# Later stages of a group woven into the absolute differences of the next

## The chip, the cores and the metric

The kernel runs on one core of a Trainium2 chip. The metric is the device time of one execution in microseconds, the median over runs; the profile is one execution of its own.

## The reference

The input is 16 images of 32 channels of 128 x 128 float32. Four layers follow one another, each of the form x = x + f(norm(x)), where norm is a group norm over pairs of channels of one image:

```python
x = x + _L0(_gn(x))   # diagonal LSTM: 128 steps along the width, state shifted by a row at each
x = x + _L1(_gn(x))   # 3x3 "adder" convolution: -sum over (c, kh, kw) of |q(patch) - q(w)|, 32 outputs
x = x + _L2(_gn(x))   # Hartley transform, 32 x 32 modes mixed over channels, inverse transform
x = x + _L3(_gn(x))   # five edge operators, each normalised over its image; conv1, pool, conv2, pool,
                      # conv3, pool, conv4, deconv, conv5, deconv, conv6, deconv, conv7; x * that
```

In L1 x and w are quantised to whole numbers from -127 to 127. In L3 `orig * y` is returned, with `orig` the normalised input.

## The kernel before

The kernel works in stages, one after another, over the whole batch; the images go through HBM between them (x1, x2, x3).

`stage0` runs the recurrence, with the batch on partitions in four groups (`NG = 4`) of four images.

`stage1` computes the absolute differences. An image is first normalised and quantised (`quantise`) to 16-bit floats in HBM (`q_d`), and loaded half by half (`loaded`, 64 rows), four copies over the partitions, so that partition = (one of 4 outputs, channel). For each half there are 72 steps `i` = (one of 8 blocks of outputs, one of 9 taps). A step makes max(q - w, 0) as a tile of 128 x 8192, on ScalarE where `i % 4 == 3` (line 365, tile `d_act`, 2 buffers), else on VectorE (line 367, `d_dve`, 4 buffers). Then 16 matmuls (line 372) with a selection matrix sum it over channels into four PSUM banks `acc`. A linear term of 9 x 16 matmuls (line 347) opens the sum of a half, since |a| = 2 max(a, 0) - a. `finish` (lines 324 and 326) adds the residual from the four banks, takes statistics and stores x2; it is called at `i == 3` of the next half. There are 4 such banks, so the linear term of a half waits for `finish` of the half before.

`stage2` is the transform: for 16 images two matmul rounds (lines 426 and 432), the modes through HBM, the mixing (line 467), through HBM again, and for each group two inverse rounds (lines 506 and 526) with the residual added in a ring of 4 tiles `xr2`.

`encoder_decoder` works by groups. `frames.chunk` loads 20 rows of x3 into a ring of 4 tiles `xp` and normalises them (line 664). `edge_statistics` forms Gram products over 128 rows (line 693) for the mean and deviation of the five operators; `fold_operators` folds the operators into conv1's weights. The function `prepared(g + 1)` stands ahead of conv1 of group g. conv1 runs 25 taps for each of 8 chunks (line 952), with pooling (line 853) and the bias into y1 (lines 862 and 864, alternately on VectorE and ScalarE); then conv2 to conv6 (lines 840 and 612), the last two composed with the deconvolutions (`Composed`). `last_layer` does the third deconvolution with conv7 (line 612 again), the scaling (lines 1032, 1041, 1044) and the output.

All instructions are emitted in the order of the program text; a scheduler then orders them per engine and places the waits. Loads go mostly through SP's queue, some stores and weights through ScalarE's.

Of the kernel before, what the change touches and what calls it, by code (L numbers as in the profile page):

```python
# [209 lines left out]
def jc_stats(nc, pool, ps, cst, v, name):  # L210

    rhs = pool.tile([128, NG, 4], F32, name=f"{name}_r")
    nc.vector.tensor_tensor(rhs, bcast(v[:, :], 2, 4), bcast(cst["m4_bc"], 1, NG), ALU.mult)
    p = ps.tile([128, 512], F32, name="acc")
    nc.tensor.matmul(p[:, :16], cst["sel_c"], rhs.rearrange("p g b -> p (g b)"), start=True, stop=True)
    out = pool.tile([128, 16], F32, name=name)
    nc.vector.tensor_copy(out, p[:, :16])
    return out


def jc_rows(t, b, half, n=16 * W):

    return bass.AP(t.tensor, t.offset + b * CHW + half * 64 * W, [[16 * W, 4], [HW, C], [1, n]])


def stage1(nc, tc, keep, cst, sel16, m1, r1, x1, w, q_d, x2):
# [8 lines left out]
    with ExitStack() as ctx:  # L235
        sm = ctx.enter_context(tc.tile_pool(name="s1_sm", bufs=1))
        with tc.tile_pool(name="s1_ps0", bufs=2, space=PSUM) as ps:
            r128 = jc_stats(nc, sm, ps, cst, r1, "r128")
            shift = jc_stats(nc, sm, ps, cst, m1, "shift")
            nc.vector.tensor_scalar(r128, r128, 128.0, None, ALU.mult)  # L240
            nc.vector.scalar_tensor_tensor(shift, shift, -1.0, r128, ALU.mult, ALU.mult)


            qw = sm.tile([128, 72], F32, name="qw")
            nc.sync.dma_start(qw, w)
            top = sm.tile([128, 1], F32, name="top")
            nc.vector.tensor_reduce(top, qw, AX.X, ALU.max, apply_absolute_value=True)
            alltop = sm.tile([128, 1], F32, name="alltop")
            nc.gpsimd.partition_all_reduce(alltop, top, 128, bass_isa.ReduceOp.max)
            scale = sm.tile([128, 1], F32, name="scale")  # L250
            nc.vector.tensor_scalar(scale, alltop, 1.0 / 127.0, 1e-8, ALU.mult, ALU.max)
            nc.vector.tensor_scalar(scale, scale, 2.0**0.5, None, ALU.mult)
            nc.vector.tensor_scalar(scale.bitcast(I32), scale.bitcast(I32), 0x7F800000, None, ALU.bitwise_and)
            nc.vector.reciprocal(scale, scale)
            nc.vector.tensor_scalar(qw, qw, scale, -127.0, ALU.mult, ALU.max)
            nc.vector.tensor_scalar(qw, qw, 127.0, RND, ALU.min, ALU.add)
            nc.vector.tensor_scalar(qw, qw, RND, None, ALU.subtract)
            neg = sm.tile([128, 72], F32, name="neg")
            nc.vector.tensor_scalar(neg, qw, -1.0, None, ALU.mult)


            taps = sm.tile([128, 8], F32, name="taps")
            nc.vector.tensor_reduce(taps, qw.rearrange("p (f t) -> p f t", t=9), AX.X, ALU.add)
            tapb = sm.tile([128, 8, 4], F32, name="tapb")
            nc.vector.tensor_tensor(tapb, bcast(taps[:, :], 2, 4), bcast(cst["m4_bc"], 1, 8), ALU.mult)
            sumw = sm.tile([128, 1], F32, name="sumw")
            p = ps.tile([128, 512], F32, name="acc")
            for j in range(4):
                nc.tensor.matmul(
                    p[32 * j : 32 * j + 32, :1],  # L270
                    tapb.rearrange("p f b -> p (f b)"),
                    cst["ones"][:, :1],
                    start=True,
                    stop=True,
                )
            nc.vector.tensor_scalar(sumw, p[:, :1], 2.0**-7, None, ALU.mult)

        stat = sm.tile([128, B, 8, 6], F32, name="stat2")
        ring = [sm.tile([128, 16, P], F16, name=f"qt{i}") for i in range(2)]
        for t in ring:  # L280
            nc.gpsimd.memset(t, 0.0)
        for row in (0, H + 1):
            nc.sync.dma_start(
                bass.AP(q_d.tensor, q_d.offset + row * P, [[4 * (H + 2) * P, 128], [(H + 2) * P, 4], [1, P]]),
                ring[0].rearrange("p r w -> p (r w)")[:, : 4 * P].rearrange("p (a w) -> p a w", w=P),
            )
        xp = ctx.enter_context(tc.tile_pool(name="s1_x", bufs=2))
        rp = ctx.enter_context(tc.tile_pool(name="s1_r", bufs=2))
        qp = ctx.enter_context(tc.tile_pool(name="s1_q", bufs=2))
        dp = ctx.enter_context(tc.tile_pool(name="s1_d", bufs=2))  # L290
        ps = ctx.enter_context(tc.tile_pool(name="s1_ps", bufs=4, space=PSUM))

        def unquantised(b, half):
            t = xp.tile([128, 16 * W], F32, name="xq")
            nc.sync.dma_start(t, jc_rows(x1, b, half))
            return t

        def quantise(b, half, t):
            nc.scalar.activation(
                t, t, AF.Identity, bias=shift[:, b : b + 1], scale=r128[:, b : b + 1]  # L300
            )
            qt = ring[half]
            nc.vector.tensor_scalar(
                qt[:, :, 1 : W + 1], t.rearrange("p (r w) -> p r w", w=W), RND, RND, ALU.add, ALU.subtract
            )
            flat = qt.rearrange("p r w -> p (r w)")
            nc.vector.tensor_scalar(flat, flat, -127.0, 127.0, ALU.max, ALU.min)
            first = q_d.offset + (b * C * (H + 2) + 64 * half + 1) * P
            nc.sync.dma_start(
                bass.AP(q_d.tensor, first, [[16 * P, 4], [(H + 2) * P, C], [1, 16 * P]]), flat  # L310
            )

        def loaded(b, half):
            q = qp.tile([128, R + 2, P], F16, name="q")
            first = q_d.offset + (b * C * (H + 2) + R * half) * P
            nc.sync.dma_start(q, bass.AP(q_d.tensor, first, [[0, 4], [(H + 2) * P, C], [1, (R + 2) * P]]))
            xr = rp.tile([128, 16 * W], F32, name="xr1")
            nc.sync.dma_start(xr, jc_rows(x1, b, half))
            return q, xr

        def finish(b, half, acc, xr):
            v = [xr[:, 512 * k : 512 * k + 512] for k in range(4)]
            for k in range(4):
                nc.vector.scalar_tensor_tensor(v[k], acc[k], sumw, v[k], ALU.subtract, ALU.add)  # L324
            for k in range(4):
                nc.vector.bn_stats(stat[:, b, 4 * half + k, :], v[k])
            nc.sync.dma_start(jc_rows(x2, b, half), xr)

        for half in range(2):
            quantise(0, half, unquantised(0, half))  # L330
        before = None
        following = loaded(0, 0)
        for b in range(B):
            for half in range(2):
                q, xr = following
                if (b, half) != (B - 1, 1):
                    following = loaded(b + half, 1 - half)
                if half == 0 and b + 1 < B:
                    xq = [unquantised(b + 1, i) for i in range(2)]
                acc = [ps.tile([128, 512], F32, name="acc") for _ in range(4)]  # L340
                for tap in range(9):
                    kh, kw = tap // 3, tap % 3
                    for j in range(4):
                        for k in range(4):
                            rows = slice(32 * k, 32 * k + 32)
                            row = 16 * j + 4 * k + kh
                            nc.tensor.matmul(  # L347
                                acc[k][32 * j : 32 * j + 32, :],
                                sel16[rows, 8, :],
                                q[rows, row : row + 4, kw : kw + W],  # L350
                                start=tap == 0,
                                stop=False,
                            )
                for i in range(72):
                    f8, tap = i // 9, i % 9
                    kh, kw = tap // 3, tap % 3
                    act = i % 4 == 3
                    if i == 3 and before:
                        finish(*before)
                    d = dp.tile([128, R, P], F16, name="d_act" if act else "d_dve", bufs=2 if act else 4)  # L360

                    src = q[:, kh : kh + R, :] if kw == 1 else q[:, kh : kh + R, kw : kw + W]
                    dst = d if kw == 1 else d[:, :, :W]
# [179 lines left out]
def replicated(nc, pool, src, n, name):  # L543
# [3 lines left out]
    return wr  # L547


class Composed:  # L550

# [44 lines left out]
    def round(self, src, n, acc, pick):  # L602
# [3 lines left out]
        for tap in range(4):  # L606
# [13 lines left out]
            if tap != 2:  # L620
                continue
# [577 lines left out]
```

## Time and profile before

| what | us |
|---|---|
| runs | 8965.4, 8966.56, 8978.64; median 8966.56 |
| profiled execution, its own time | 8964.56 |
| its span, first to last instruction | 8962.7 |
| stage0 and first quantisation, to the first difference | 0 to 1510 |
| absolute differences | 1510 to 5697 |
| transform | to 6450 |
| encoder and decoder | to 8558 |
| last layer | to 8962.7 |
| busy PE, DVE, ACT, POOL | 6114.4, 5850.7, 5003.2, 268.8 |

PE is TensorE, PEld its weight loads, DVE is VectorE, ACT ScalarE, POOL GpSimd, SP the engine that issues most DMAs. A group of the profile names the line, the engine, the operation, output and input tiles, the count, the busy time and mean duration, and what ended the idle time before it.

### The profile page before, as it was taken

The numbers are of one execution on the slowest core, as the hardware profiler recorded it, in microseconds if no ns is written. First come the engines' busy times: TensorE is split into PE (matmuls) and PEld (weight loads), VectorE is DVE, ScalarE is ACT, GpSimd is POOL, SyncE is SP. The second block draws the span as 40 slices with busy tenths as digits, with TensorE's granted clock in tenths as the row PEclk, the third lists the DMA queues.
The fourth block names the chain that finished last, engine by engine and source line by source line (L and its number), as shares of the span: only waits on it lengthen the run. The fifth ranks groups of instructions, "written<-read, shape, count | busy, mean of one in ns | idle before, by whom it ended". The sixth has DMA issues, their size and how long they took to land.

```text
span 8962.7 us, 249632 instructions
## 1 busy us (share of the span) xinstructions
PE 6114.4 (68%) x117740; PEld 4037.0 (45%) x117740; DVE 5850.7 (65%) x5842; ACT 5003.2 (56%) x2710; POOL 268.8 (3%) x483
## 2 busy tenths in 40 slices
PE   4999991666666656665665666784656859678955
PEld 3888881222222222222222223584644646455832
DVE  5444432999999999999999999622633232232233
ACT  1444432999999999999999999400000101101122
POOL 0111110000000000000000000000000000000000
PEclk9999995999999999999999999755556859688977
DMA  9799923111111111111111110344721121211077
GB/s 205 53 80 78 82 24 80 42 46 42 42 51 54 44 44 52 39 43 48 54 49 43 41 40 25 121 101 115 244 67 43 37 59 43 59 34 34 27 184 170
DMA packets 1520672, 613.85 MB, mean 68 GB/s; under 512 B 1418269, under 2 KB 1421725, under 8 KB 1491613
## 3 DMA queue, kind: packets, MB, share of 16 engines
q1 hardware_dynamic: 1480636, 518.56, 31.2%
q10 hardware_dynamic: 39008, 79.32, 3.0%
q8 instruction: 922, 15.11, 0.7%
q14 instruction: 106, 0.86, 0.0%
HBM read 433.21 MB, written 164.64 MB: 67 GB/s over the span
## 4 chain that ended last, share of the span: by engine, by line
issue 41%; PE 37%; DVE 14%; ACT 3%; DMA 3%; SPq 1%; another core or an unknown queue 0%; POOL 0%; ACTq 0%; DVEq 0%; POOLq 0%
PE acc L952 10%; DVE d_dve L367 7%; PE pg L174 5%; PE pg L175 4%; PE acc L693 4%; PE acc L612 3%; PE pg L176 3%; PE p L426 2%; ACT d_act L365 2%; PE acc L840 2%; PE pf L526 1%; DVE xr L324 1%; DVE stat L200 1%; PE pa L506 1%; PE p L432 1%
## 5 line engine op out<-in xcount | busy, mean ns | idle before, releaser
L365 ACT ACTIVATE d_act<-q,neg 128x8192 f16<-128x8192 f16 (+1 forms) x576 | 4065.9, 7150 | 54.7 <-PE acc L372 29.9
L367 DVE TENSOR_SCALAR d_dve<-q,qw 128x8192 f16<-128x8192 f16 (+1 forms) x1728 | 3935.0, 2365 | 55.6 <-PE acc L372 32.6
L372 PE MATMUL acc<-d_dve,sel 128*32 128x512 f16 x27648 | 1854.7, 391 | 1317.7 <-DVE d_dve L367 1315.9
L372 PEld LDWEIGHTS <-sel 128*32 128x32 f16 x36864 | 1077.8, 98 | 2786.0 <-issue 2082.7
L952 PE MATMUL acc<-xp,fo_all 32*32 32x512 f32 x25600 | 932.4, 624 | 53.1 <-DVE pooled L853 48.5
L952 PEld LDWEIGHTS acc<-xp,fo_all 32*32 32x32 f32 x25600 | 661.4, 105 | 313.7 <-issue 157.5
L372 PE MATMUL acc<-d_act,sel 128*32 128x512 f16 x9216 | 648.0, 401 | 161.5 <-ACT d_act L365 161.1
L185 ACT ACTIVATE gt<-pg,bias 128x256 f32<-128x256 f32 x1024 | 400.9, 474 | 547.5 <-PE pg L176 547.4
L174 PE MATMUL pg<-h,bd 128*128 128x256 f32 x2048 | 652.7, 401 | 57.8 <-DVE h L194 57.5
L175 PE MATMUL pg<-h,bd 128*128 128x256 f32 x2048 | 623.4, 387 | 0.0
L864 ACT ACTIVATE y<-pooled,fo_b 32x128 f32<-32x128 f32 x256 | 102.4, 400 | 842.8 <-DVE pooled L853 839.4
L980 DVE TENSOR_TENSOR acc<-acc,cut 128x4 f32<-128x4 f32 x256 | 28.7, 166 | 696.4 <-PE acc L952 695.4
L693 PE MATMUL acc<-xp 32*32 32x108 f32 x16384 | 326.8, 376 | 222.1 <-issue 217.1
L176 PE MATMUL pg<-xn,bd 128*128 128x2 f32 (+62 forms) x2048 | 426.1, 289 | 9.6 <-DVE xn L158 9.6
L176 PEld LDWEIGHTS pg<-xn,bd 128*128 128x128 f32 x2048 | 397.2, 194 | 66.8 <-DVE xn L158 10.4
L175 PEld LDWEIGHTS pg<-h,bd 128*128 128x128 f32 x2048 | 398.3, 194 | 56.9
L189 DVE TENSOR_TENSOR c<-c,gt 128x256 f32<-128x256 f32 x256 | 108.6, 424 | 448.7 <-ACT gt L185 448.7
L664 DVE TENSOR_SCALAR xp<-xp,stats 128x2560 f32<-128x2560 f32 (+1 forms) x64 | 101.0, 1580 | 446.9 <-DMA xp<-x_d 446.9
L693 PEld LDWEIGHTS acc<-xp 32*32 32x32 f32 x16384 | 250.4, 134 | 298.8 <-issue 271.1
L174 PEld LDWEIGHTS pg<-h,bd 128*128 128x128 f32 x2048 | 341.9, 195 | 64.7 <-issue 48.4
L347 PE MATMUL acc<-q,sel 32*32 32x512 f16 x4608 | 183.8, 594 | 228.6 <-DVE xr L324 135.0
L669 ACT COPY xp<-xp 128x20 f32<-128x20 f32 x64 | 14.9, 233 | 554.6 <-DVE xp L664 442.8
(234 smaller groups left out, 4693.7 us busy)
## 6 DMA issues: line engine op xcount, KB each, us to landing
xr<-x_d SPq DMA_DIRECT2D x96, 1024.0 KB
q<-q_d SPq DMA_DIRECT2D x32, 2145.0 KB
xp<-x_d SPq DMA_DIRECT2D x48, 1280.0 KB
x_in<-in_x_dram SPq DMA_DIRECT2D x16, 2048.0 KB
res<-in_x_dram SPq DMA_DIRECT2D x32, 1024.0 KB
x_d<-res SPq DMA_DIRECT2D x32, 1024.0 KB
xq<-x_d SPq DMA_DIRECT2D x32, 1024.0 KB
x_d<-xr SPq DMA_DIRECT2D x32, 1024.0 KB
```

Of the source, the lines that this page charges most:

```text
L174: nc.tensor.matmul(pg[:, q], wmat(0, q), h_in[:, :, 1:], start=True, stop=False)
L175: nc.tensor.matmul(pg[:, q], wmat(1, q), h_in[:, :, :H], start=False, stop=False)
L176: nc.tensor.matmul(pg[:, q, :, : t + 1], wmat(2, q), xn[:, 2 * c : 2 * c + 2, j, : t + 1], start=False, stop=True,)
L185: nc.scalar.activation(gt[:, q], pg[:, q], AF.Tanh if q == 3 else AF.Sigmoid, bias=bias[:, q : q + 1])
L347: nc.tensor.matmul(acc[k][32 * j : 32 * j + 32, :], sel16[rows, 8, :], q[rows, row : row + 4, kw : kw + W], start=tap == 0, stop=False,)
L365: nc.scalar.activation(dst, src, AF.Relu, bias=neg[:, i : i + 1])
L367: nc.vector.tensor_scalar(dst, src, qw[:, i : i + 1], 0.0, ALU.subtract, ALU.max)
L372: nc.tensor.matmul(acc[k][32 * j : 32 * j + 32, :], sel16[:, f8, :], d[:, row : row + 4, c : c + W], start=False, stop=i == 71,)
L426: nc.tensor.matmul(p1[:, i, :], xh[:, 16 * half + i, :], cst["cas"], start=True, stop=True)
L612: nc.tensor.matmul(acc[blk][32 * j : 32 * j + 32, : rows * n], self.w[part, par, tap, :], src[part, top : top + rows, left : left + n], st ...
L693: nc.tensor.matmul(gram[blk][32 * j : 32 * j + 32, at : at + 36 * n], xp[rows, l, 2 + 32 * j : 34 + 32 * j], xp[rows, l : l + n, 32 * j : ...
L952: nc.tensor.matmul(acc[blk][32 * j : 32 * j + 32, :], wf["all"][rows, tap, :], xp[rows, 4 * j + kh : 4 * j + kh + 4, kw : kw + W], start=t ...
```

## The change

The batch order is turned: after the recurrence everything else runs in one function `rest`. The differences (class `Differences`) go image by image as before. The later stages (class `After`) go group by group as one Python generator, `work`, which emits a few instructions and then yields: a positive number is a price in us of TensorE time, a negative one a time to hold back what follows, a tuple names the image that must be stored first. A class `Weave` keeps the account: `dve` and `act` are summed prices of what was emitted on the two engines, their mean is `now`; `credit` is TensorE time left over. After each step of the differences `advance` lets the generator go on while there is credit and no hold; closures put in by `later` are emitted once `now` has reached their time. What is left of the generator after the last image is emitted by `drain`. `keep_order` makes each instruction of the woven part depend, on its own engine, on the one emitted before it.

In the woven part:

- the choice between ScalarE and VectorE follows the account, for 3 <= i < 68 only; the sums of a ScalarE tile are emitted 4 or more steps later; `d_dve` has 3 buffers for 4; the linear term and the first three sums are emitted at i == 3, behind `finish` of the half before, and steps 0 to 2 let nothing of the generator in;
- quantisation goes in four quarters of 8 rows, the residual in two tiles loaded at i == 40;
- the later stages have 4 PSUM banks `acc`, the other 4 belong to the differences;
- once per run, `prepare` composes the three deconvolutions and builds tables of the folded operators (`fold`), both kept in HBM and reloaded for each group;
- the transform is done for 4 images at a time; its mixing has N = 4 for 16, with 8 weight tiles `mix` of 1 MB read again for each group, and contraction over 64 partitions; `xr2` and `xh` have 2 buffers; copies go to VectorE;
- frames are normalised on ScalarE, in a ring of 3 for the statistics and of 2 for conv1; conv1's bias goes to ScalarE, that of conv2 to conv5 to VectorE, that of conv6 to ScalarE; the Gram weights are read per operator;
- the last layer goes by quarters of 32 rows; all DMAs of `rest` are issued by SP, GpSimd does only the preparation of the differences.

The core of the diff. It shows, in order, `Weave`, `rest`, one half in `Differences.run`, `After.work`, the Gram products of the statistics, and conv1:

```diff
+class Weave:
+    def __init__(self, work):
+        self.work, self.pending = work, None
+        self.now = self.credit = self.hold = self.dve = self.act = 0.0
+        self.finished, self.count, self.put_off = -1, 0, []
...
+    def step(self):
+        v = self.pending or next(self.work, None)
+        self.pending = None
+        if v is None:
+            return False
+        if isinstance(v, tuple):
+            if v[1] > self.finished:
+                self.pending = v
+                return False
+        elif v < 0:
+            self.hold = -v
+        else:
+            self.credit -= v
+            self.spent = v
+        return True
+
+    def advance(self, pe):
+        us = (self.dve + self.act) / 2 - self.now
+        self.now += us
+        self.credit = min(self.credit + us - pe, 5.0)
+        self.hold = max(self.hold - us, 0.0)
+        self.due(self.now)
+        if self.credit < 2.0:
+            return
+        while self.credit > 0 and not self.hold and self.step():
+            pass
...
+DVE_US, ACT_US, PE_US = 2.28, 7.1, 0.87
+
+def rest(nc, tc, cst, sel16, bias, m1, r1, a, d, out):
...
+        start = len(nc.cur_bb.bb.instructions)
+        first.run(tc, ctx, weave)
+        keep_order(nc, tc, start)
+        weave.drain()
...
-                q, xr = following
...
-                acc = [ps.tile([128, 512], F32, name="acc") for _ in range(4)]
...
+                q = following
+                late, ahead, xq = [], [], {}
+                for i in range(72):
+                    if i == 3:
+                        if before:
+                            self.finish(*before)
+                        acc = [ps.tile([128, 512], F32, name="acc1") for _ in range(4)]
+                        self.linear(acc, q)
+                        for t, n in ahead:
+                            self.sums(acc, t, n)
+                    if i == 8 and (b, half) != (B - 1, 1):
+                        following = self.loaded(b + half, 1 - half)
...
-                    act = i % 4 == 3
-                    d = dp.tile([128, R, P], F16, name="d_act" if act else "d_dve", bufs=2 if act else 4)
+                    act = weave.act + ACT_US < weave.dve + DVE_US and 3 <= i < 68
+                    t = dp.tile([128, R, P], F16, name="d_act" if act else "d_dve", bufs=2 if act else 3)
...
                     if act:
+                        nc.scalar.activation(dst, src, AF.Relu, bias=self.neg[:, i : i + 1])
+                        weave.act += ACT_US
+                        late.append((acc, t, i))
                     else:
+                        nc.vector.tensor_scalar(dst, src, self.qw[:, i : i + 1], 0.0, ALU.subtract, ALU.max)
+                        weave.dve += DVE_US
+                        while late and (i - late[0][2] > 3 or i == 71):
+                            self.sums(*late.pop(0))
+                        if i < 3:
+                            ahead.append((t, i))
+                            continue
+                        self.sums(acc, t, i)
+                    weave.advance(PE_US * (4 if i == 3 else 1))
...
+    def work(self):
+        yield from self.prepare()
+        for g in range(NG):
+            with self.tc.tile_pool(name="g_sm", bufs=1) as sm:
+                yield ("after", 4 * g + 3)
+                yield -15.0
+                self.stats3 = sm.tile([128, 2, 1], F32, name="stats3")
+                yield from self.transform(g, sm)
+                yield from self.encoder(g)
+                yield from self.last(g, sm)
...
+        yield -40.0
+        gram = [self.acc() for _ in range(4)]
+        for ch in range(H // 16):
+            weave.done(ready)
+            for l in range(2, 18):
...
+                yield 0.6
+            if ch + 3 < H // 16:
+                yield -3.0
+                chunks[ch % 3] = load(ch + 3)
...
+                xp, ready = chunks[ch % 2]
+                weave.done(ready)
...
+                    yield 1.15
+                yield -4.5
+                if ch + 2 < H // R:
+                    chunks[ch % 2] = load(ch + 2)
...
+                weave.later(6.0, spread)
+                yield -2.0
```

Other prices and holds of one group: a transform round 1.2 per 4 channels, mixing 1.6 per column of modes, first inverse 0.8 and second 2.0 per round, `take_out` adds 2.8 to `dve`; a load of a frame is normalised 20 us later; up-sampling and conv2 to conv4 cost 1.0 per 512 columns and 0.15 a tap; a unit of the last layer holds 4.5 and 13 per half, and a group ends on a hold of 50.

## The prediction

> **What bounds the kernel now.** The slices of the page come first: each character is 1/40 of the span, 224 us.
>
> ```profile
> PE   4999991666666656665665666784656859678955
> ...
> DVE  5444432999999999999999999622633232232233
> ACT  1444432999999999999999999400000101101122
> ...
> PEclk9999995999999999999999999755556859688977
> DMA  9799923111111111111111110344721121211077
> ```
>
> Three regimes: the recurrence (slices 0 to 6), the absolute differences (DVE and ACT at 9, PE at 6), and the later stages, with ACT near 0, DVE at 2 to 3 and a PE clock that falls to 0.5. The busy time by stretch sizes them (columns: stretch, us, busy of PE, PEld, DVE, ACT, POOL, granted clock, DMA share, GB/s).
>
> ```profile
> 1510.00:5692.00 4182.00, 2567.51 (x41460) 1182.94 (x41464) 4141.00 (x2049) 4122.26 (x605) 0.00 (x0) 0.94 0.15 44
> 5692.00:6450.00 758.00, 540.90 (x10524) 515.36 (x10516) 285.63 (x361) 32.42 (x45) 0.00 (x0) 0.50 0.55 161
> ...
> 8558.00:8962.70 404.70, 229.42 (x5676) 114.49 (x5676) 131.18 (x174) 89.00 (x128) 0.00 (x0) 0.74 0.84 195
> ```
>
> The differences are bound by DVE and ACT alone, both 99% busy; PE has some 1,600 us idle. The later stages (758 of transform, 2,108 of encoder, 405 of last layer) are latency and PE. The groups by line give the durations.
>
> ```profile
> L365 ACT ACTIVATE d_act<-q,neg 128x8192 f16<-128x8192 f16 (+1 forms) x576 | 4065.9, 7150 | 54.7 <-PE acc L372 29.9
> L367 DVE TENSOR_SCALAR d_dve<-q,qw 128x8192 f16<-128x8192 f16 (+1 forms) x1728 | 3935.0, 2365 | 55.6 <-PE acc L372 32.6
> ```
>
> The timeline at a change of half shows what follows the last difference.
>
> ```profile
> 2976.54 2.72 DVE L324 SCALAR_TENSOR_TENSOR xr<-acc,sumw,xr 128x512 f32<-128x512 f32 x4
> 2977.34 6.00 PE L347 MATMUL acc<-q,sel 32*32 32x512 f16 x144 [3.56 <-DVE xr L324]
> ...
> 2979.18 2.46 DVE L326 BATCH_NORM_STATS2 stat<-xr 128x6 f32<-128x512 f32 x4
> ...
> 2981.55 2.37 DVE L367 TENSOR_SCALAR d_dve<-q,qw 128x8320 f16<-128x8320 f16 x1
> ```
>
> DVE ends `finish` at 2981.6 and goes straight into a fourth `d_dve` buffer, though PE is in the linear term until 2983.3. And two lines of the statistics:
>
> ```profile
> 6495.74 2.54 PE L693 MATMUL acc<-xp 32*32 32x108 f32 x128 [1.04 <-issue]
> 6499.21 2.54 PE L693 MATMUL acc<-xp 32*32 32x108 f32 x128 [0.93 <-issue]
> ```
>
> 128 matmuls with their 128 weight loads take 3.47 us: 0.87 us a row of 64 instructions; with longer gaps the 128 rows of group 0 took 133.8 us (6492.8 to 6626.6), 1.04 a row.
>
> **What the Trainium skill says.** "TensorE: Matmul & The Clock Gate", on the array's architecture: ScalarE and VectorE take instructions strictly in order, and only weight loads overtake on PE. So one late matmul holds all behind it; the trace agrees, PE's waits being for the difference next in order. The same page, on the clock gate: after an idle window the PE clock halves. The trace agrees: 0.50 in 2976 to 2984 after 3.56 us of waiting, 0.97 after it. "DMA: Bandwidth & Descriptors", on issuing engines: queues of different engines share the same 16 DMA engines. So moving ACT's DMAs to SP should cost only issue time, 0.58 us each for `xp` here; no run here compares queues.
>
> **The change, part by part.** I work against the profiled execution: span 8962.7, its own time 8964.6, 2.0 below the median 8966.6.
>
> *Head.* The recurrence and first quantisation stay: the first difference starts at 1510. Four half-size quantisations for two move equal bytes: 0, +-15.
>
> *Foreground.* 16 images in 1510 to 5697: 4,187. A whole image costs 259.4 (128.1 and 131.3 a half). The account's prices agree: DVE ran 14 in 31.93 us (2.28), ACT 5 in 35.41 (7.08), 16 matmuls 0.86.
>
> *Added to DVE and ACT.* Increments in the diff for one group: DVE 83+28+18+31+34+32 = 226 (transform, statistics, fold, conv1, small layers, last), ACT 6+29+0+84+14+38 = 172 (rounded); they fit the rows: centring 4.42 against 4.3, pooling 0.69 against 0.65. As the account splits differences so that both engines end together, a us on either costs half a us.
>
> *How much is woven.* A step costs (7.1 x 2.28)/(7.1+2.28) = 1.73 us, PE 0.87 of it, so half of each us is PE credit, capped at 5 us: long holds lose it. A stretch then lasts price/0.5 + holds. Transform to conv1: 490 us of price, 526 of holds: 1,506. Small layers and last: 90 and 355: 535. Group 0 may start once image 3 is stored, 1,076 us in, and ends at 3,117; group 1's conv1 ends at 4,623. The foreground ends near then. So **1.7 groups are woven, not three**: small layers and last of group 1, and groups 2 and 3 whole, run in the drain. Added work woven: group 0 398/2 = 199; group 1 to conv1 279/2 = 140; operator tables 146 x 0.25/2 = 18. Together 357: foreground 4,544.
>
> *Stalls in it.* (a) Three `d_dve` buffers: the next difference waits for the first sum, 2983.27+0.86 = 2984.1, where DVE is free at 2981.6: 2.5 a half. ACT gets nothing in i<3 and i>=68, then three operations in a row, the third blocked by two buffers; its room to lag absorbs most. I take 4 a half for both: 130, bounds 50 and 300. (b) PE prices: a gram row is 0.6 and takes 0.87 to 1.04, 35 to 56 a group; the linear term (6.0 a half) is in no price; conv1 at 1.15 a tap runs 28.89 for 25. Where PE is filled, DVE waits: 120, bounds 40 and 250. (c) Some 45 hand-overs a group from PE to DVE behind holds of 4.5, against bursts of up to 5: 80, bounds 0 and 300. (d) ACT in order behind loads; `xp` is issued at 6507.4 and used at 6514.6, 7 us, against 20 allowed, but beside loads of 2 MB more: 60, bounds 0 and 250. (e) Square roots between Relu, instruction fetch beside more DMA, uncounted small operations: 60, bounds 20 and 200. Sum 450; none can be a gain, as the engines were full. SP passes a load only when the buffer's last reader is done; `q` has 64 steps of lead, so it costs nothing unless SP lags by 110 us.
>
> *The drain.* One group alone, with 4 PSUM banks and few buffers. Transform: loads 20, then 4 images at 19 (17.1 a PE round, 10.85+3.17+1.9 and so on, plus the DVE hop): 96; to DRAM and back 18; mixing 2,048 matmuls at 28 ns (4,096 took 115): 57, with weight loads 65; back through DRAM 22; first inverse 42 (36 plus copies on DVE only, 1.08 each); second inverse 72, since with two `xr2` buffers 5.6 of DVE, a store and a load (9.05 seen) follow each other; statistics 10: 325, against 758/4 = 190. Statistics and fold 134+10+34+35+20 = 233 (gram as seen, first load, reductions, tables, edge sums), against 192 in 7710 to 7902. Conv1 8 x 34 = 272, against 265 in 7375 to 7640. Small layers 122, against 70 after it, spreading on one engine. Last layer 104 at the old rate, plus 26 for the y6 round trip and 20 for start and end: 150. Sum 1,102; pool hand-overs 20: **1,120 a group** against 817 (3,270/4), bounds 950 and 1,250. Drain: 122+150+2 x 1,120 = 2,512.
>
> *Sum.* 1,510 + 4,544 + 450 + 2,512 = 9,016 span; with 1.9 outside and 2.0 to the median, **9,020**. Hidden: 1.7 groups; paid: 357+450 in the foreground, 600 in the drain. Break-even: stalls and drain together 2,909; I have 2,962.
>
> **Rivals.** *Faster: the weave keeps its account.* Stalls at about their lower bounds (200; all lower bounds sum to 110) and 950 a group in the drain (272+1,900): 8,426. For: the prices of the two bound engines match the rows. Against: it needs holds written for a full pipeline to cost nothing when empty. This rival covers 8,400 to 8,945: 0.38. *Much slower: in-order coupling.* A matmul late behind an ACT result holds the sums of `d_dve`, and three buffers give DVE only 4.6 us. From 7 us of lateness on at every hand-over (45 a group, 77 in all at 1.7 groups, and the 32 halves), 109 x 7 = 760 come in place of 210 for (a) and (c): 9,570. For: both bound engines are 99% busy, so nothing is caught up. Against: PE would be filled only in conv1 and gram. 0.18. *It weaves nothing:* if steps stayed behind their gates, 1,510+4,187+4 x 1,120 = 10,177; the gates are images finished long before: 0.02.
>
> **How the numbers follow.** Forecast, 8,985 to 9,300: 0.36. Within 0.2% (18 us, about what a measurement of this kernel can tell from no change): 0.06. Slower cases 0.36+0.18+0.02 = 0.56, faster 0.38. Both signs hold much, so the forecast's own range, 8,985 to 9,300, stands beside the whole one, 8,450 to 9,700, which leaves out the ends of the rivals.
>
> **What would show it.** Right: ACT and DVE at 9 until about 6,500, PE at 8 to 9 in the second half of that; then some 2,500 us with ACT near 0, two conv1 blocks in it, and a PE clock down to 0.5. (a) shows as DVE waiting for PE after `finish`, 2.5 us times 31. Wrong: three conv1 blocks or one after the last difference (the account's reach), a drain group under 1,000 us, or a foreground end before 6,200 or after 6,900.

## The result, and the profile after

| kernel | median, us | ratio to before (95%) |
|---|---|---|
| before | 8971.6 | |
| changed | 9105.2 | 1.015 (1.0133 to 1.0168) |

The changed kernel is slower by 134 us. The forecast was slower by 53 (9,020). The profiled execution of the changed kernel has a span of 9113.6; it was the longest of the four, some 10 us above their median.

The slices of its page, of 228 us each, answer to those of before:

```profile
PE   4999983666667667688766776758875548664585
...
DVE  5444445999998788788888887888872221122212
ACT  2444434899998798788798888878862012110122
...
PEclk9999996888988788899888777879986558765696
DMA  9999953111022331211133233221104331144204
```

The plateau of DVE and ACT now ends in slice 29, not 24 (counted from 0), and stands mostly at 7 and 8 where it stood at 9: the two bound engines idle wherever the later stages are woven in (from slice 12 on). PE stands at 5 to 8 there, where it was at 5 or 6, and what is left behind the plateau is ten slices, where it was fifteen. The stretches give the numbers (columns as before: busy PE, PEld, DVE, ACT, POOL, granted clock, DMA share, GB/s).

```profile
1485.00:6771.00 5286.00, 3760.11 (x77146) 1838.14 (x77150) 4567.14 (x3274) 4511.30 (x1098) 0.00 (x0) 0.85 0.22 68
6771.00:9113.60 2342.60, 1458.74 (x43590) 1054.79 (x43582) 496.05 (x1243) 382.62 (x606) 0.00 (x0) 0.66 0.32 89
```

Differences: 5,286 for 4,182. Of the 1,104 added, work is 408 (DVE's busy time +426, ACT's +389, mean), and idle time 697: DVE idles 719 for 41, ACT 775 for 60. Behind them 2,343 remain, for 3,271. The groups by line name what the idle time waits for (last columns: idle time before the group, and what ended most of it).

```profile
L536 ACT ACTIVATE d_act<-q,neg 128x8192 f16<-128x8192 f16 (+1 forms) x592 | 4196.7, 7153 | 776.0 <-PE acc L463 732.5
L540 DVE TENSOR_SCALAR d_dve<-q,qw 128x8192 f16<-128x8192 f16 (+1 forms) x1712 | 3936.9, 2357 | 582.6 <-PE acc L463 547.7
L463 PE MATMUL acc<-d_dve,sel 128*32 128x512 f16 x27392 | 2000.0, 430 | 709.1 <-DVE d_dve L540 696.7
```

Before, the last of these groups was:

```profile
L372 PE MATMUL acc<-d_dve,sel 128*32 128x512 f16 x27648 | 1854.7, 391 | 1317.7 <-DVE d_dve L367 1315.9
```

The differences themselves cost what they cost before (7,153 and 2,357 ns). Before, DVE waited 32.6 us for sums (then line 372) to free a buffer; now it waits 548, and ACT 733. In the same stretch PE still waits 697 us for DVE's tiles (1,316 before, when it had only the differences). So PE isn't full in the mean: each side waits for the other in turn. The Trainium skill, "Perfetto Trace Analysis", Optimization Strategy, says that a gap which repeats on the engine that ought to be full can mean too few buffers; the trace shows such a gap, 194 waits of DVE, but no run here has more buffers, so whether they would close it is not shown.

**How far the weave got** is as forecast. The conv1 taps alone (line 1375) by stretch:

```profile
6173.00:6752.00 579.00, 234.51 (x6400) 104.33 (x6400) 0.94 0.14 40
7551.00:7802.00 251.00, 236.22 (x6400) 159.59 (x6400) 0.94 0.13 34
```

The first is group 1, ending at 6,752, 19 us ahead of the end of the differences (6,771); the second is group 2, in the drain. A conv1 that is woven stretches from 251 to 579 us, with the same PE time.

**What a wait looks like.** The timeline, in conv1 of group 0, PE and then DVE:

```profile
3892.70 1.05 PE L463 MATMUL acc<-d_dve,sel 128*32 128x512 f16 x16
3893.67 5.58 PE L1375 MATMUL acc<-xp,wf 32*32 32x512 f32 x160
3899.18 1.05 PE L463 MATMUL acc<-d_act,sel 128*32 128x512 f16 x16
3900.06 1.91 PE L463 MATMUL acc<-d_dve,sel 128*32 128x512 f16 x32
```
```profile
3893.80 2.35 DVE L540 TENSOR_SCALAR d_dve<-q,qw 128x8192 f16<-128x8192 f16 x1 [2.60 <-PE acc L463]
3901.16 4.65 DVE L540 TENSOR_SCALAR d_dve<-q,qw 128x8320 f16<-128x8320 f16 x2 [5.01 <-PE acc L463]
```

The account has let five taps in at once (160 matmuls, 5.58 us). DVE had waited 2.60 us already; one difference fits into the buffer that had just come free, the other two buffers hold tiles that are not summed yet. Then DVE stands for 5.01 us, until the sums behind the five taps have freed one. Of three buffers one is being written, so at best two more differences, 4.7 us, can follow while PE is elsewhere.

Conv1 is the plain case, but not the whole. Its two woven stretches hold some 155 of the 548 us; the rest lies in the other woven stages and at the heads of the halves. In the statistics ten rows of Gram products followed one another without a sum between them; two lines of PE, then one of DVE:

```profile
3426.20 1.76 PE L1092 MATMUL acc<-xp 32*32 32x108 f32 x128 [2.09 <-issue]
3429.95 1.76 PE L1092 MATMUL acc<-xp 32*32 32x108 f32 x128 [1.99 <-issue]
...
3435.39 2.35 DVE L540 TENSOR_SCALAR d_dve<-q,qw 128x8192 f16<-128x8192 f16 x1 [6.42 <-PE acc L463]
```

Priced at 6.0 us, the ten rows kept PE from 3,423.2 to 3,434.3, and DVE stood 6.42 us. In the differences, 75 of the 308 stretches of woven work that no sum interrupts were longer than 4.7 us from their first start to their last end, the longest 19.7.

### The profile page after: what moved, and what is told of

The parts are those of the page before. It is cut to its first block, busy times and chain, and to the rows that moved or that the text cites. A ratio compares the mean times of both kernels' runs of the same rounds, so it can differ in the third digit from the quotient of the medians.

```text
span 9113.6 us, 267984 instructions
## 1 busy us (share of the span) xinstructions
PE 6416.4 (70%) x126892; PEld 3970.8 (44%) x126892; DVE 5713.2 (63%) x5908; ACT 5410.8 (59%) x2993; POOL 229.3 (3%) x263
## 5 line engine op out<-in xcount | busy, mean ns | idle before, releaser
L536 ACT ACTIVATE d_act<-q,neg 128x8192 f16<-128x8192 f16 (+1 forms) x592 | 4196.7, 7153 | 776.0 <-PE acc L463 732.5
L540 DVE TENSOR_SCALAR d_dve<-q,qw 128x8192 f16<-128x8192 f16 (+1 forms) x1712 | 3936.9, 2357 | 582.6 <-PE acc L463 547.7
L463 PE MATMUL acc<-d_dve,sel 128*32 128x512 f16 x27392 | 2000.0, 430 | 709.1 <-DVE d_dve L540 696.7
L463 PEld LDWEIGHTS <-sel 128*32 128x32 f16 x36864 | 1120.4, 106 | 2640.7 <-issue 2028.1
L463 PE MATMUL acc<-d_act,sel 128*32 128x512 f16 x9472 | 766.5, 450 | 459.4 <-ACT d_act L536 451.2
L1375 PE MATMUL acc<-xp,wf 32*32 32x512 f32 x25600 | 943.0, 621 | 18.6 <-DVE pooled L1300 17.8
L1375 PEld LDWEIGHTS acc<-xp,wf 32*32 32x32 f32 x25600 | 525.2, 105 | 375.7 <-issue 244.2
L1314 ACT ACTIVATE y<-pooled,b 32x128 f32<-32x128 f32 x512 | 204.6, 400 | 400.2 <-DVE pooled L1300 393.2
L1092 PE MATMUL acc<-xp 32*32 32x108 f32 x16384 | 285.3, 326 | 185.9 <-issue 161.8
L680 PE MATMUL acc<-y6l,u_conv 32*32 32x256 f32 x8192 | 284.6, 475 | 123.6 <-issue 75.3
L1092 PEld LDWEIGHTS acc<-xp 32*32 32x32 f32 x16384 | 222.9, 120 | 258.1 <-issue 214.4
```

The lines of the kernel that those rows point to most:

```text
L463: self.nc.tensor.matmul(acc[k][32 * j : 32 * j + 32, :], self.sel16[:, i // 9, :], d[:, row : row + 4, c : c + W], start=False, stop=i == 71,)
L536: nc.scalar.activation(dst, src, AF.Relu, bias=self.neg[:, i : i + 1])
L540: nc.vector.tensor_scalar(dst, src, self.qw[:, i : i + 1], 0.0, ALU.subtract, ALU.max)
L680: nc.tensor.matmul(acc[blk][32 * j : 32 * j + 32, o : o + rows * n], t[part, 4 * par + tap, :], src[part, top : top + rows, left : left + ...
L1092: nc.tensor.matmul(gram[blk][32 * j : 32 * j + 32, at : at + 36 * n], xp[rows, l, 2 + 32 * j : 34 + 32 * j], xp[rows, l : l + n, 32 * j : ...
L1314: nc.scalar.activation(d, s, AF.Identity, bias=bj)
```

## The experiments

Times are medians, each ratio is to the kernel before on the same chip, whose median lay between 8,950 and 8,979; "idle" is DVE's idle time before the instructions of the differences. It includes the wait for the first load of `q`, which lies ahead of the first difference (23 us before, 29 to 35 in the others); without it the changed kernel's 753 are the 719 above. The runs lie on several chips, so what one run gains on another is taken from the ratios, or from the columns of the trace.

| kernel | time | ratio to before (95%) | differences | idle | waits for a `d_dve` buffer | after them |
|---|---|---|---|---|---|---|
| before | | | 4,181 | 61 | 33 | 3,271 |
| changed | 9,105 | 1.0133 to 1.0168 | 5,285 | 753 | 548 | 2,343 |
| e1 nothing let in | 9,913 | 1.1025 to 1.1058 | 4,858 | 559 | 227 | 3,574 |
| e2 room 1.2 | 9,006 | 1.0017 to 1.0040 | 5,067 | 549 | 424 | 2,460 |
| e3 prices | 9,148 | 1.0173 to 1.0203 | 5,152 | 647 | 470 | 2,506 |
| e4 long holds halved | 9,126 | 1.0150 to 1.0181 | 5,422 | 857 | 590 | 2,214 |
| e5 nothing let in, ordered | 10,248 | 1.1423 to 1.1461 | 4,403 | 282 | 243 | 4,356 |
| e6 room 1.0 | 8,967 | 1.0003 to 1.0017 | 5,000 | 491 | 346 | 2,491 |
| e7 room 1.0, credit 40 | 8,976 | 1.0013 to 1.0027 | 5,125 | 591 | 402 | 2,368 |
| e8 no order | 9,824 | 1.0958 to 1.0993 | 6,007 | 1,496 | 708 | 2,332 |
| e9 = e5, linear term spread | 10,167 | 1.1346 to 1.1380 | 4,311 | 192 | 152 | 4,367 |
| e10 = e6, linear term spread | 8,905 | 0.9937 to 0.9970 | 4,932 | 424 | 281 | 2,483 |
| e11 linear term spread | 9,025 | 1.0071 to 1.0101 | 5,201 | 670 | 481 | 2,337 |
| e12 sums 6 steps later | 9,112 | 1.0156 to 1.0186 | 5,288 | 754 | 520 | 2,342 |
| e13 = e10, 6 steps | 8,945 | 0.9976 to 0.9990 | 4,969 | 460 | 283 | 2,481 |

**Lumps, order or prices.** Theory 1: PE falls behind because the woven work comes in lumps longer than the buffers cover. Theory 2: engines held to the order of emission wait behind late results. Theory 3: PE's time is over-committed, since Gram rows and the linear term cost more than their prices.

`e1_no_weave` lets nothing in:

```diff
-        if self.credit < 2.0:
-            return
-        while self.credit > 0 and not self.hold and self.step():
-            pass
+        return
```

> The account lets nothing of the later stages in during the differences; all of them run in the drain, in the new order. It sizes the differences' own new form and a drain group. From the profile of the changed kernel: the halves in which nothing was woven took 132 to 137 us for 128 to 131 before, so 16 images should take some 4,290 for 4,187; groups 2 and 3 took 1,042 and 1,039 in its drain, so four groups take 4,160, and the preparation some 150: 1,485 + 4,290 + 4,310 = 10,085 in all. If the differences take 4,400 or more here, the stalls belong to their new form and not to the weaving; if a group takes less than 1,000 or more than 1,080, the drain groups of the changed kernel aren't typical.

It missed, 9,913 for 10,085: what `drain` emits is not chained, so the scheduler itself moved group 0 ahead into the differences (its conv1 begins at 5,680, where the differences end at 6,343). It does not size the base; `e5` below does.

`e2_paced` limits what one step of the differences lets in:

```diff
-        if self.credit < 2.0:
-            return
-        while self.credit > 0 and not self.hold and self.step():
-            pass
+        room = 1.2
+        while self.credit > 0 and room > 0 and not self.hold:
+            self.spent = 0.0
+            if not self.step():
+                break
+            room -= self.spent
```

> The same account and the same holds, but each step of the differences lets in about 1.2 us of TensorE price at most (one tap of conv1, two Gram rows), in place of all the credit at once, up to 5 us from 2 on. Theory 1 (lumps: PE falls behind because the woven work comes in lumps longer than the 4.6 us that three d_dve buffers cover): DVE's idle time in the differences falls from 740 to about 500, the foreground from 5,287 to about 5,090; about a quarter of conv1 of group 1 moves to the drain, +60: 8,970. Theory 2 (order: DVE and ACT wait behind late results of the woven part) and theory 3 (PE has too little time in all, because Gram rows, linear term and taps cost more than their prices): idle time unchanged, the drain +60: 9,165.

(A room of 1.2 lets a second tap in, 2.3 us, not one. The edit also drops the threshold of 2 us of credit.) Idle 549 and differences 5,067 are near theory 1's 500 and 5,090; the drain grew by 117, not 60, so a part of the gain is that less was woven.

`e3_priced` sets `yield 0.95` for a Gram row and adds 6.0 to the price of step 3.

> A Gram row is priced 0.95 for 0.6 and the linear term of a half 6.0 for nothing; lumps stay as they are. Theory 3 (PE has too little time because of unpriced work): DVE's idle time falls from 740 to about 550, and with +50 in the drain (a fifth of conv1 of group 1) the time is about 8,965. Theory 1 (lumps): only the lumps of Gram rows shrink, idle falls by some 60: 9,095. Theory 2 (order): 9,155.

Idle fell by 106, between theory 1's 60 and theory 3's 190, and the drain grew by 163, more than the 50 that I had reckoned. The prices are too low, but to correct them only trades weaving for idleness: 9,148 is no gain.

`e4_long_holds_half`:

```diff
-            self.hold = -v
+            self.hold = -v if v > -20.0 else -0.5 * v
```

> Holds of 20 us and more (waits for loads and for the end of a group, some 245 us a group) are halved, so that more is woven: by the account the foreground ends in the small layers of group 1 and not at the end of its conv1. If the holds were longer than needed: drain shorter by 100, foreground longer by some 40 for the added work: 9,045. Theory 2 (order: what is let in too early stops an engine until its load has come): stalls grow by 100 or more and DVE's waits for DMA rise from about 70 to 150: 9,150 or more.

The drain fell by 129 and the differences grew by 137, of it 104 idle. Theory 2's growth of the stalls came, its cause did not: DVE's waits for DMA (without the first load) rose only from 66 to 88, not to 150, so late loads are not what stands behind it.

**What the new form costs by itself.** `e5_none_ordered` is `e1` with `keep_order` called after `drain`:

> As the run that let nothing in, but the order of emission is kept to the end, so that no instruction of the drain can be moved ahead into the differences, as happened there with group 0 (282 us of DVE's idle time waited for its DMAs). Differences alone in their new form: 16 images at 268 = 4,290, DVE's idle time about 165 at half boundaries (5 a half) and 35 at the first load; if it is 400 or more, the new form itself stalls, and what paced lumps left (549) isn't from the weaving. Drain: four groups at 1,040 and the preparation 150; if a strictly ordered group takes over 1,080, the order of emission costs by itself. In all 10,085.

It was slower than forecast by 160: the differences alone took 4,403, of which DVE waits 243 us for buffers, and a group 1,055 (the first transforms of the groups begin at 6,048, 7,095, 8,156 and 9,213), some 15 more than in the changed kernel's drain, where the order is not kept. A half's head in this kernel, PE, then ACT, then DVE:

```profile
3142.17 5.97 PE L476 MATMUL acc<-q,sel 32*32 32x512 f16 x144 [5.58 <-DVE xr L443]
3148.07 2.79 PE L460 MATMUL acc<-d_dve,sel 128*32 128x512 f16 x48
3150.68 1.04 PE L460 MATMUL acc<-d_act,sel 128*32 128x512 f16 x16
...
3159.00 1.90 PE L460 MATMUL acc<-d_act,sel 128*32 128x512 f16 x16 [4.09 <-ACT d_act L533]
3160.66 1.51 PE L460 MATMUL acc<-d_dve,sel 128*32 128x512 f16 x16
3166.02 1.90 PE L460 MATMUL acc<-d_act,sel 128*32 128x512 f16 x16 [3.84 <-ACT d_act L533]
```
```profile
3113.32 28.37 ACT L533 ACTIVATE d_act<-q,neg 128x8192 f16<-128x8192 f16 x4
3151.83 28.27 ACT L533 ACTIVATE d_act<-q,neg 128x8192 f16<-128x8192 f16 x4 [10.15 <-PE acc L460]
```
```profile
3169.67 6.91 DVE L537 TENSOR_SCALAR d_dve<-q,qw 128x8192 f16<-128x8192 f16 x3 [5.06 <-PE acc L460]
```

PE waits 5.58 us for `finish`, then runs the linear term for 5.97. ACT, ahead of the others, has filled both its buffers by 3,141.7, and stands 10.15 us until the first of them is summed. Its later tiles are late by this, PE waits for them in order (4.09, 3.84), and DVE stands 5.06 us behind that at 3,169.7. Of DVE's 243 us of waits for a buffer, 221 begin within 30 us of a half's `finish`.

This run also takes the change apart (spans): the new form alone costs 10,243.8 - 8,962.7 = 1,281, of which 222 in the differences and 1,085 in the stages after them, which now go group by group, less 25 at the head. Some 60 of the 1,085, 15 a group, go with the order kept in this run's drain, by estimate. Weaving 1.7 groups then gains 1,130: 2,013 taken from the drain for 882 added to the differences.

**Finer lumps.** `e6_paced_one` is `e2` with `room = 1.0`; `e7_paced_cap40` adds `min(self.credit + us - pe, 40.0)`.

> Room 1.0 for 1.2 in a step of the differences: one tap of conv1 (1.15) at a time, where 1.2 let a second one in, so lumps of 1.15 for 2.3. Theory 1 (lumps): DVE's idle time falls on from 549 to about 480, the foreground to about 5,000; two fifths of conv1 of group 1 are left to the drain, +40 against room 1.2: about 8,980. If lumps under the 4.6 us of the buffers no longer matter, idle stays at 550 and the time is about 9,040.

> As room 1.0, but credit is kept up to 40 us for 5, so that what holds let lapse is used afterwards, at one tap a step: 0.87 + 1.15 = 2.03 us of PE for a step of 1.73. By the account nine tenths of conv1 of group 1 are then woven for six: drain shorter by about 75. Theory 3 (PE is full where it is given more than its share): idle grows by the 15% overdraft in gram and conv1, about 100: 9,005. If PE's time is not the limit, idle stays and the time is 8,910, below the kernel before.

`e6` met theory 1's numbers (491, 5,000, 8,967). Its timeline in conv1, PE and then DVE:

```profile
3882.57 1.14 PE L1377 MATMUL acc<-xp,wf 32*32 32x512 f32 x32
3883.64 1.05 PE L465 MATMUL acc<-d_dve,sel 128*32 128x512 f16 x16
3884.62 1.15 PE L1377 MATMUL acc<-xp,wf 32*32 32x512 f32 x32
3885.69 1.05 PE L465 MATMUL acc<-d_dve,sel 128*32 128x512 f16 x16
```
```profile
3882.69 18.29 DVE L542 TENSOR_SCALAR d_dve<-q,qw 128x8320 f16<-128x8320 f16 x8 [0.36 <-PE acc L465]
```

One tap, one set of sums, 2.05 us a pair on a full PE, and DVE runs eight differences in a row: here PE does have the time. `e7` wove more than `e6`, and paid for it what it gained: drain -123, differences +125, idle +100, theory 3's forecast in amount.

`e7` is also the run to set beside the changed kernel, since it weaves nearly as much (drain 2,368 for 2,343) at the same prices, only in small pieces (its threshold and cap of credit differ too): 7 of its 714 stretches of woven work are over 4.7 us, for 75 of 308. Its waits for a buffer (total, times, longest) fall from 548:

```profile
DVE d_dve L542 <- PE acc L465: 402.0, 217, 13.5
```

So 146 us of these waits go with the lumps, and theory 1 holds for that part. The further fall to 346 in `e6` goes with weaving less, since the two differ in the cap alone.

**The order of emission.** `e8_no_order` leaves the call of `keep_order` out.

> The changed kernel without the chain of order: the scheduler places the woven part by its own rule. Theory 2 (the order of emission is what costs: engines wait behind late results though other work is ready): idle time falls by 200 or more, 8,900. Theory 1 (lumps): as the scheduler follows the text unless an operand is late, the lumps stay, 9,105 within 50. If the scheduler breaks up the account (as in the run that let nothing in, where it spread group 0 over 3,900 us), 9,300 or more.

The order itself is not the cost that theory 2 took it for: without it the kernel is some 730 us slower, and the third case of the expectation came (9,300 or more). DVE idles 1,496 us; three of the waits, DVE's and then ACT's (total, times, longest):

```profile
DVE d_dve L539 <- PE acc L462: 708.3, 215, 45.0
...
DVE qt L419 <- DMA q_d<-qt: 338.2, 17, 54.0
...
ACT xq L412 <- DMA xq<-x_d: 768.0, 38, 62.0
```

A quantisation stands up to 54 us for a store on SP's queue to free its buffer, and up to 62 for its load. In all, waits for DMA in the differences (without the first load) grow from 66 to 521 us on DVE and from 7 to 871 on ACT. The woven stretches on PE are not coarser than in the changed kernel (65 of 464 over 4.7 us). That engines wait in order behind late results this run does not refute: the half head of `e5` shows such waits.

**The linear term.** Three kernels take it from the head of a half: the first sums open the banks (`start=i == 0`), and

```diff
-                        self.linear(acc, q)
...
+                    if 12 <= i < 21:
+                        self.linear(acc, q, [i - 12])
```

`e9_none_spread` does this to `e5`, `e10_one_spread` to `e6`, `e11_spread` to the changed kernel.

> The ordered run that lets nothing in, with the linear term taken from the head of a half: the first sums open the banks, and one tap of the linear term is emitted at each of steps 12 to 20. It left 282 us of DVE's idle time, 244 of it for d_dve buffers; in its trace PE waits 5.6 us for finish and then runs the linear term for 6.0, and ACT, whose two buffers wait for sums behind that, stands 10 us (251 a run), which throws DVE 20 us later. If the 6 us of the linear term in front of the sums are the cause: ACT's wait falls to 3 to 4 us a half, DVE's idle time by 150, the differences from 4,403 to 4,250, and the time to 10,095. If finish itself or three buffers are the cause: unchanged, 10,245.

> Both: one tap at a time (8,967) and the linear term spread over steps 12 to 20. DVE's idle time was 491, ACT's 542, of which 347 in the second 10 us of a half. If the two causes add up, idle falls by some 170 more, and the time to about 8,800, under the kernel before. If the lateness at the head of a half was hidden behind the woven part's own waits: 8,930 or more.

> The changed kernel with its lumps of up to 5 us, and only the linear term spread: 9,105 less some 160, 8,945, if the head of a half and the lumps are separate causes; within 50 of 9,105 if lumps make PE late there anyway.

All three gained, by the ratios some 70, 50 and 60 us (the differences alone 92, 67 and 84), a third to a half of what I expected. The gain is of like size with and without weaving, so this cause is mostly separate from the lumps. ACT at the head of a half in `e9` still stands 7.00 us for 10.15:

```profile
3115.55 21.26 ACT L534 ACTIVATE d_act<-q,neg 128x8192 f16<-128x8192 f16 x3 [7.00 <-PE acc L460]
```

The wait for `finish` in front of the first sums stays (190 us of PE's waits in all, 186 in `e5`). With both changes `e10` is faster than the kernel before, by half a per cent: 8,905 against 8,950 in the same comparison, ratio 0.9954 (0.9937 to 0.9970).

**Later sums for ScalarE.** `e12_late6` and `e13_one_spread_late6` have `i - late[0][2] > 5` for `> 3`.

> The changed kernel with one number changed: the sums of a ScalarE tile are emitted 6 or more steps later for 4. Four steps are 4 x 1.73 = 6.9 us, less than the 7.15 that ScalarE takes, so that PE, in order, waits for ScalarE's tile (451 us in all in the changed kernel's groups) while VectorE's sums stand behind. If this wait is a third cause of VectorE's idle time: 753 falls by 150 and the time to about 8,960. If PE is late by lumps and the linear term anyway, the wait is only slack: 9,105 within 30; if ScalarE's two buffers come free too late then, its idle time (809) grows, and the time is 9,150 or more.

> One tap at a time, the linear term spread, and 6 steps for 4: 424 us of VectorE's idle time were left at 8,905, 109 of them in the third 10 us of a half, where PE waits for a late ScalarE tile with VectorE's sums behind it (4.6 and then 5.8 us in the run that let nothing in). If that is the cause: idle falls by 100 to 150, and the time to about 8,790. If not: 8,905 within 30.

No gain: in `e12` PE's wait for ACT tiles falls from 451 to 403, and ACT's wait for its buffers rises from 733 to 751; in `e13` ACT's rises from 405 to 466, and the time by the ratios by some 26 us (forecast: faster by some 115, or unchanged within 30). The wait only changes sides. What makes up the 424 us of idle time that `e10` still has (389 without the first load) is not settled; some 170 of it begin 10 to 30 us behind the start of `finish`. A fourth `d_dve` buffer wasn't tried, so whether it would help, or fit beside the tiles of the later stages, is open.

## Why the prediction was wrong

Its structure held, and one term of the sum was mis-sized; two errors partly cancelled.

- *Head*: 1,485 for 1,510, -25, outside the +-15 that I gave it.
- *Added work in the foreground*: 357 forecast, 408 measured, +51.
- *How much is woven*: 1.7 groups, conv1 of group 1 ending where the differences end: by the account it was to end 79 us behind them (4,623 for 4,544), and it ended 19 ahead, with two conv1 blocks in the drain as forecast. This rested on the account alone.
- **Stalls**: 450 forecast, 697 measured. This is the step that failed, in two of its five parts.
- *(b) PE behind, the larger miss*: 120 forecast from what the prices leave out. DVE's waits for a buffer are 548, less the 243 that `e5` has with nothing woven in: 305. I priced an average overrun, and put the length of a single insertion at nothing: I had noted bursts of up to 5 us under the hand-overs and buffers for 4.6 us under the rivals, and had not set the one against the other. `e7` shows it: nearly the same weave at the same prices, in pieces, waits 402 - 243 = 159. So 146 us go with the lumps. The 159 that are left are of the size that I had given (b); that they are what the prices leave out is not shown.
- *(a) The head of a half*: 130 forecast, 204 in `e5` (mean of DVE 206 and ACT 202 over before), inside the bounds of 50 and 300. I had written that ACT's room to lag absorbs most of it; the trace shows that ACT is ahead, not behind, and its two buffers are what stops it.
- (c) Hand-overs, 80 forecast: DVE's waits for PE other than for its buffers are 74. (d) Loads, 60: 66 for DMA. Both held. (e), 60, has no measure of its own; some 50 of the 697 are left for it.
- *Drain*: 2,512 forecast, 2,343 measured, -169. A group took 1,040 (7,033 to 9,113.6 for two) for 1,120: in group 2 the transform 292 for 325, statistics and fold 226 for 233, conv1 251 for 272, the rest 273 for 292. The rest of group 1 took 262 for 272. This hid two thirds of the error in the stalls. That is luck: the two were reckoned apart.
- Sum against 9,016: -25 - 5 (base 4,182 for 4,187) + 51 + 247 - 169 = +99, that is 9,115, and 9,113.6 was measured.

Of the rivals, the one of in-order coupling had the right mechanism with 7 us at every hand-over; the coupling is there, 2.8 us a time in the mean of 194 waits, but at the lumps and half heads. The rival that the account is kept failed on the stalls, and on the drain too (1,040 a group for its 950). The signs held in part: (a) showed as DVE waiting for PE after `finish` (2.7 us at the head shown of `e5`), but 133 of its 221 us came 10 to 30 us later, at that head through ACT; DVE and ACT did not stay at 9, and PE stood at 5 to 8, not at 8 to 9.

The Trainium skill, "TensorE: Matmul & The Clock Gate", on the array's architecture, says that ACT and DVE take instructions strictly in order and that on PE only weight loads are pulled ahead. The traces agree: in `e5` the sums of DVE's next tile stood behind the 4.09 us that PE waited for ACT's. With what the same page says of the clock gate the trace agrees too: the two sets of 16 matmuls that took 1.90 us in `e5` came after some 4 us of waiting, at a granted clock of 0.50 (3,159 to 3,161), and a set took about 1.05 at 1.00 (3,148 to 3,155).

## What to carry to other kernels

When work is woven into a stretch that two engines fill, the mean share of the third engine is not enough; set the longest single insertion against what the buffers between the engines cover in time, and insert one piece per step. Here that took 146 us of buffer waits away at nearly the same weave, not all of them. Before weaving, price what the new form costs with nothing woven in: here it was 1,281 us, more than the weave gave back. Near balance a further us woven costs a us in the foreground (`e4`, `e7`), so the gain is in the stalls, not in weaving more.

## What the runs showed that was not expected

- The granted clock in the differences fell from 0.94 to 0.85 although PE had more to do; a matmul of DVE's sums took 430 ns for 391. With nothing woven in it was already 0.88. Why is open.
- Gram products that ran in blocks of 128 matmuls every 3.47 us before came every 3.75 in the weave (3,426.20, 3,429.95), with gaps of 2.0 us for 0.93 that no semaphore explains.
- Without the chain of order the scheduler's own placement of the same instructions took some 730 us more; with nothing woven it moved one group into the differences by itself, and that was some 350 us faster than the ordered form.
